# Rows of a block renumbered over the four column tiles of the product with Wu, and the gate's loads issued by GpSimd

## The chip, the cores and the metric

The kernel runs on one core of a Trainium2 chip. Times are device microseconds (us) of that core. A core has a matrix engine (TensorE, PE in the profile; its weight loads are PEld), VectorE (DVE), ScalarE (ACT), GpSimd (POOL) and SyncE (SP). Each engine takes its instructions in the order in which the program lists them. DMA transfers are issued by SyncE, ScalarE or GpSimd. The result of a matmul goes to PSUM; ScalarE or VectorE must read it out before the buffer can be used again.

## The reference

The input x is (32, 8, 256, 256): 32 images of 8 channels. Four layers follow each other, each `x = x + f(group_norm(x))` with 4 groups of 2 channels. The first layer has nearly all the work:

```python
grid = drive                                   # the normalised image
for _ in range(15):
    mapped = 3.9 * grid * (1.0 - grid)
    local = conv3x3(mapped, K_local, groups=8)  # one 3x3 kernel per channel
    grid = 0.85 * (0.7 * mapped + 0.3 * local) + 0.15 * drive
cml = clip(grid, 1e-4, 1 - 1e-4)
h   = relu(conv3x3(x, Wp, bp))                  # 8 -> 128 channels
nca = sigmoid(conv1x1(h, Wu, bu))               # 128 -> 8
g   = sigmoid(conv1x1(relu(conv3x3([x, cml, nca], Wg1, bg1)), Wg2, bg2))
f   = g * cml + (1 - g) * nca
```

Layer 1 is a 3x3 convolution of values rounded to 8 bits, with one scale taken over the whole batch; layer 2 is a 3x3 convolution in float32; layer 3 averages 5x5 windows. All is float32 except the products of layer 1.

## The kernel before

**Two stages.** Layer 0 runs first, for all images, because the scale of layer 1 needs the maximum over the batch; its result goes to `x1_d` in device memory. Layers 1 to 3 follow, image by image, three images in flight.

**Layer 0, the lattice.** `lattice(b, ahead)` makes the 15 steps for image b. Six channels (`CP`) are kept as patches of 16 x 8 pixels on the partitions, in two halves of three channels. A half-step is: three matmuls with `patch_sb` (L367), three with `ring_sb` on the neighbouring patches' edges (L369), then on VectorE a step to take the result out of PSUM (L377) and one to form `v * (v - 1)` (L383), and four DMAs (`spread`, L245, SyncE) that copy the edges to `rings`. The other two channels are computed on VectorE alone: they lie in `strip`, four rows to a partition, and nine multiply-adds (`tap`, L316) form the 3x3 sum. Six of the nine (dy = 1 and 0) stand in the first half-step and three (dy = 2) in the second; at its end `own`, the inner rows of `strip`, is written (L395) and two DMAs (`edges`, L249 and L250) bring the rows above and below from the neighbours. The `psc` results share three PSUM buffers.

**Layer 0, the rest.** `gated()` makes the 128-channel product, the one with Wu, and the gate. An image is cut into 16 blocks of 16 rows, and one n stands for two blocks (row r of both, 512 columns, in one matmul), so an image has eight n. `load(n, half)` brings `im`, eight rows with their neighbours, in six DMAs by GpSimd (L474); two `im` buffers are used. A batch is four rows: four matmuls `ph` with `wp_sb` (L602), each taken out by ScalarE as `hh` (L607). After the second `ph` of the next batch, `second()` multiplies those four `hh` with Wu (L580, `pn`). Each of these products has 32 output columns, of which 8 are not zero: row r goes to the 32 partitions of column tile q, at place i within it, with `q, i = divmod(r, 4)`. In the order (0, 4, 1, 5) the four products of a batch use the tiles 0, 1, 0, 1. After 16 rows `close` applies the sigmoid (`nh`, L558) and loads `hb`, the rows next to the block's border, by `beside_blocks`.

`gate(n, quarter)` is cut into pieces, and each batch runs the next piece of each gate that is due. The first piece issues the loads, on ScalarE's queue: `xq` and `cq` (L486) and `ha` (`beside_blocks`, L451) for every second n, `xc` (L492, two DMAs) for each n. Then come three pieces of six `pg` instructions (L506), one with `ha` and `hb` (L511, L512) and a relu, one with `pq` (L517) and a sigmoid, and one with seven VectorE operations and the store of the result (L539, GpSimd).

**The order of the work.** It is written out by hand (`manual_schedule`). `lattice(b)` yields after each half-step a length of time (`BLOCK`, 7.4), and as much of `gated()` of image b − 1, by the lengths that this yields, is put there. After each half-step one item of `errands` follows: stores of the normalised image (`xn_d`, `nr_d`), loads of the next one, and its statistics in the pieces of `stats_parts`. Image 0 has no `gated()` beside it, and that of image 31 stands alone at the end.

**Layers 1 to 3.** The order there is chosen by the framework. `layer2` stores its result to `x3` (L740) and loads it again as `y`, in other places, with 16 DMAs (L747); `layer1` of a later image loads `x1` (L703). All of these are issued by GpSimd.

## Time and profile before

| what | value |
|---|---|
| median of 3 runs | 17682.97 us (17682.23 to 17724.92) |
| profiled execution, own time | 17729.61 us |
| profiled execution, span | 17727.6 us |
| PE busy | 16666.2 us (94%) |
| PEld busy | 6752.9 us (38%) |
| DVE busy | 13279.5 us (75%) |
| ACT busy | 4005.7 us (23%) |
| POOL busy | 2761.8 us (16%) |
| granted TensorE clock, mean | 0.953 |

A line of a group names the source line, the engine, the operation, the tiles written and read, the shapes and the count; then the busy time in us and the mean length in ns; then the time that the engine stood idle just before, and what ended it. Idle time of an engine that is not the bottleneck costs nothing. In the list of waits the numbers are the total in us, the count, and the longest. In a timeline the columns are the start, the length (both us), the engine and the instruction, and in brackets the idle time before it. "ACTq" and "SPq" are the queues' own instructions, DMA issues above all; on POOL the issues are shown as busy time. In the answer by stage the columns are the stretch, its length, the busy time of PE, PEld, DVE, ACT and POOL with the number of instructions, the granted clock, the DMA engines' share and GB/s.

### The profile page before, as it was taken

The page shows a single profiled execution, that of the slowest core. Times are in us where ns is not written, and L with a number is a line of the kernel's source. Part 1 is how long each engine was busy: PE and PEld are TensorE (multiplying, and loading weights), DVE is VectorE, ACT ScalarE, POOL GpSimd, SP SyncE. Part 2 cuts the span into 40 slices and gives each one's busy share as a digit, 9 for nine tenths or more (in the row PEclk, how much of TensorE's full clock was granted, in tenths as well). Part 3 has the DMA queues.
Part 4 walks back from the last instruction along what each step waited for, and adds up shares of the span by engine and source line. Part 5 has one row for each costly group of instructions (what it writes and reads, how often), then busy time and mean ns, then how long its engine had stood idle before and what let it go on. Part 6 is the DMA issues. An engine that isn't in the chain of part 4 may idle for free.

```text
span 17727.6 us, 134114 instructions
## 1 busy us (share of the span) xinstructions
PE 16666.2 (94%) x42888; PEld 6752.9 (38%) x42888; DVE 13279.5 (75%) x17529; ACT 4005.7 (23%) x5982; POOL 2761.8 (16%) x4469
## 2 busy tenths in 40 slices
PE   5999999999999999999999999999999999899999
PEld 2333333333333333333333333333333333344444
DVE  8787777777777887777888777787777885555554
ACT  0222222222222222222222222222222222211110
POOL 0111111111111111111111111111111111111111
PEclk7999999999999999999999999999999999899999
DMA  4666666666666666666666666666666665455554
GB/s 82 125 124 129 128 128 125 126 128 127 129 125 126 131 123 129 124 124 126 127 126 127 130 127 130 128 129 124 131 127 128 128 122 117 113 124 125 131 126 103
DMA packets 846207, 2208.34 MB, mean 125 GB/s; under 512 B 251021, under 2 KB 529781, under 8 KB 761413
## 3 DMA queue, kind: packets, MB, share of 16 engines
q0 software_dynamic: 341504, 1147.07, 33.4%
q1 hardware_dynamic: 352452, 774.38, 21.4%
q10 hardware_dynamic: 151552, 278.31, 6.0%
q8 instruction: 350, 5.73, 0.2%
q14 instruction: 349, 2.85, 0.1%
HBM read 1078.72 MB, written 404.28 MB: 84 GB/s over the span
## 4 chain that ended last, share of the span: by engine, by line
PE 73%; DVE 14%; DMA 9%; issue 2%; ACTq 1%; ACT 1%; POOL 0%; SPq 0%; DVEq 0%; POOLq 0%
PE ph L602 16%; PE psc L367 11%; PE psc L369 11%; PE pg L506 10%; PE pn L580 7%; DVE acc L316 7%; PE psv L771 6%; PE psv L692 5%; DMA strip<-strip 3%; DVE state L383 2%; DVE state L377 2%; DMA ha<-nr_d 2%; PE psv L696 2%; DMA rings<-state 1%; PE psv L775 1%
## 5 line engine op out<-in xcount | busy, mean ns | idle before, releaser
L316 DVE SCALAR_TENSOR_TENSOR acc<-strip,taps_sb,acc 128x1024 f32<-128x1024 f32 x3840 | 4930.8, 1284 | 359.6 <-DMA strip<-strip 243.2
L602 PE MATMUL ph<-im,wp_sb 72*128 72x512 f32 x8192 | 4190.5, 626 | 580.4 <-ACT hh L607 530.8
L607 ACT ACTIVATE hh<-ph,bp_sb 128x512 f32<-128x512 f32 x4096 | 2753.5, 687 | 7094.7 <-PE ph L602 6611.3
L377 DVE SCALAR_TENSOR_TENSOR state<-psc,flat 128x512 f32<-128x512 f32 x2880 | 1900.6, 686 | 2022.1 <-PE psc L369 1736.8
L367 PE MATMUL psc<-state,patch_sb 128*128 128x512 f32 x5760 | 2817.8, 626 | 261.2 <-DVE stat L105 154.2
L369 PE MATMUL psc<-rings,ring_sb 80*128 80x512 f32 x5760 | 2704.8, 606 | 24.4 <-DMA rings<-state 24.2
L474 POOL DMA_DIRECT2D im<-xn_d x3072 | 1726.4, 567 | 5667.5 <-PE ph L602 5580.7
L602 PEld LDWEIGHTS ph<-im,wp_sb 72*128 72x128 f32 x8192 | 1494.1, 194 | 2693.2 <-issue 1872.2
L580 PE MATMUL pn<-hh,wu_sb 128*32 128x512 f32 x8192 | 1979.2, 604 | 0.0
L367 PEld LDWEIGHTS psc<-state,patch_sb 128*128 128x128 f32 x5760 | 1110.3, 199 | 1882.2 <-issue 1145.0
L383 DVE SCALAR_TENSOR_TENSOR state<-state 128x512 f32<-128x512 f32 x2688 | 1689.3, 684 | 0.0
L369 PEld LDWEIGHTS psc<-rings,ring_sb 80*128 80x128 f32 x5760 | 1116.7, 194 | 1466.8 <-issue 1443.0
L771 PE MATMUL psv<-xr,w_sb 128*128 128x512 f32 x2560 | 1160.3, 595 | 0.5 <-DVE xr L756 0.5
L539 POOL DMA_DIRECT2D x_d<-xc x256 | 146.8, 574 | 6493.9 <-DVE xc L534 6493.7
L580 PEld LDWEIGHTS pn<-hh,wu_sb 128*32 128x32 f32 x8192 | 389.1, 109 | 1438.1 <-issue 1438.1
L506 PE MATMUL pg<-xq,wg_sb 128*128 128x512 f32 x1536 | 897.5, 731 | 0.0
L692 PE MATMUL psv<-xh,w_sb 128*128 128x512 f32 x1536 | 703.3, 594 | 8.1 <-DVE xh L728 4.1
L506 PE MATMUL pg<-nh,wg_sb 128*128 128x512 f32 x1536 | 701.3, 592 | 0.0
L506 PE MATMUL pg<-cq,wg_sb 128*128 128x512 f32 x1536 | 701.2, 592 | 0.0
L771 PEld LDWEIGHTS psv<-xr,w_sb 128*128 128x128 f32 x2560 | 475.5, 189 | 565.6 <-issue 561.2
L780 DVE TENSOR_TENSOR y<-psv,y 128x512 f32<-128x512 f32 x256 | 176.5, 690 | 621.6 <-PE psv L775 621.5
L316 DVE SCALAR_TENSOR_TENSOR acc<-strip,taps_sb,d 128x1024 f32<-128x1024 f32 x480 | 613.7, 1278 | 0.0
(147 smaller groups left out, 10893.0 us busy)
## 6 DMA issues: line engine op xcount, KB each, us to landing
im<-xn_d POOLq DMA_DIRECT2D x3072, 193.3 KB, 8.2
rings<-state SPq DMA_DIRECT2D x1920, 159.5 KB
rings<-state SPq DMA_DIRECT2D x1920, 106.3 KB
strip<-strip SPq DMA_DIRECT2D x960, 126.0 KB
xn_d<-xb POOLq DMA_DIRECT2D x128, 516.0 KB, 12.5
nr_d<-xb POOLq DMA_DIRECT2D x128, 516.0 KB, 12.0
xq<-nr_d ACTq DMA_DIRECT2D x128, 516.0 KB
cq<-cr_d ACTq DMA_DIRECT2D x128, 516.0 KB
```

The costliest lines, as they stand in the source:

```text
L316: nc.vector.scalar_tensor_tensor(acc, strip[:, dy : dy + RQ, dx : dx + W], taps_sb[:, 3 * dy + dx : 3 * dy + dx + 1], d2 if dy == 1 and dx ...
L367: nc.tensor.matmul(pss[-1], patch_sb[:, c, :], inner(c), start=True, stop=False)
L369: nc.tensor.matmul(pss[c % HALF], ring_sb[:, c, :], rings[half][:, c % HALF, 0 : TX * SY].rearrange("p (x y) -> p x y", y=SY)[:, :, 0:TY], ...
L377: nc.vector.scalar_tensor_tensor(inner(c), pss[c % HALF], FLOOR, dr[:, c], ALU.max, ALU.add)
L383: nc.vector.scalar_tensor_tensor(v, v, 1.0, v, ALU.subtract, ALU.mult)
L474: nc.gpsimd.dma_start(im[24 * dy : 24 * dy + 24, k, 0:run], window(xn_d[b % 3], at, [[HP * WP, C], [1, 3], [1, run]]),)
L506: nc.tensor.matmul(o, wg1_sb[:, s, dx, :], src[:, :, dx : dx + W], start=s == dx == 0, stop=False,)
L580: nc.tensor.matmul(pn[32 * q : 32 * q + 32, :], wu_sb[:, i, :], hh, start=i == 0, stop=i == 3,)
L602: nc.tensor.matmul(ph.rearrange("p (k w) -> p k w", w=W), wp_sb, im[:, :, j * WP : j * WP + W], start=True, stop=True,)
L607: nc.scalar.activation(hh, ph, AF.Relu, bias=bp_sb)
L692: nc.tensor.matmul(o, w[:, dx, :], src[:, 2 * i : 2 * i + 2, dx : dx + W], start=dx == 0, stop=False,)
L771: nc.tensor.matmul(o, w3_sb[:, dx, :], xr[:, k, 2 * g : 2 * g + 2, dx : dx + W], start=dx == 0, stop=False,)
```

## The change

The rows of a block are numbered anew: row r now goes to column tile r mod 4, at place r // 4 (`i, q = divmod(r, 4)`), and a batch is four rows in turn, so that its four products with Wu name all four column tiles. Everything that is laid out by rows follows: the stores to `nr_d` and `cr_d`, the loads of `xc` and `y`, which now take four rows 4 apart in a DMA, and the weights of the convolutions over rows (`turn`). The gate's loads go from ScalarE's queue to GpSimd's, `beside_blocks` among them. `load` is issued in pieces among the matmuls of the next batch. The taps with dy = 0 go to the second half-step. `stats_parts` pauses once more, before the square root.

```diff
@@ stats_parts
         nc.vector.tensor_scalar(u[:, 0:1], ps2[:, 0:1], 1e-5, None, ALU.add)
+        yield
         nc.scalar.activation(u[:, 1:2], u[:, 0:1], AF.Sqrt)
@@ errands (cr_d in lattice likewise)
-                            nr_d[b % 3], r.start * C * HB * WP,
-                            [[WP, P], [C * HB * WP, 4], [1, WP]],
+                            nr_d[b % 3], r.start // 4 * C * HB * WP,
+                            [[WP, P], [4 * C * HB * WP, 4], [1, WP]],
@@ lattice
-                    for dy in (1, 0) if half == 0 else (2,):
+                    for dy in (1,) if half == 0 else (0, 2):
@@ beside_blocks
-                    nc.scalar.dma_start(
+                    nc.gpsimd.dma_start(
@@ load
+                ims.append(im)
                 for dy in range(3):
                     for k in range(2):
...
+                        yield
-                ims.append(im)
@@ gate
-                        nc.scalar.dma_start(quarter[name], t[b % 3][:, k0 : k0 + 4, :])
+                        nc.gpsimd.dma_start(quarter[name], t[b % 3][:, k0 : k0 + 4, :])
...
                 for k in range(2):
-                    nc.scalar.dma_start(
-                        xc[:, k, :],
-                        window(
-                            x, b * C * H * W + (k0 + k) * RB * W, [[W, RB], [H * W, C], [1, W]]
-                        ),
-                    )
+                    for j in range(4):
+                        at = b * C * H * W + ((k0 + k) * RB + j) * W
+                        nc.gpsimd.dma_start(
+                            xc[32 * j : 32 * j + 32, k, :],
+                            window(x, at, [[4 * W, 4], [H * W, C], [1, W]]),
+                        )
@@ second
-                    q, i = divmod(r, 4)
+                    i, q = divmod(r, 4)
@@ gated
-                    for rows in ((0, 4, 1, 5), (2, 6, 3, 7)):
+                    for rows in ((0, 1, 2, 3), (4, 5, 6, 7)):
...
                             four.append((hh, 8 * half + j))
+                            next(coming, None)
+                            if i % 2 == 0:
+                                next(coming, None)
...
-                    if n + 1 < B * NCH:
-                        load(n + 1, half)
+                    coming = load(n + 1, half) if n + 1 < B * NCH else iter(())
@@ layer2
             for k in range(HB):
-                nc.gpsimd.dma_start(
-                    y[RB * (k % 8) : RB * (k % 8) + RB, k // 8, :, :],
-                    window(x3, k * W, [[C * NPX, RB], [NPX, C], [1, W]]),
-                )
+                for i in range(4):
+                    m = RB * (k % 8) + 4 * i
+                    nc.gpsimd.dma_start(
+                        y[m : m + 4, k // 8, :, :],
+                        window(x3, i * C * NPX + k * W, [[4 * C * NPX, 4], [NPX, C], [1, W]]),
+                    )
@@ laid_out, on_rows
-        return a.reshape(RB * i, 3, RB * o)
+        turn = np.arange(RB) % 4 * 4 + np.arange(RB) // 4
+        return a[turn][:, :, :, turn].reshape(RB * i, 3, RB * o)
```

## The prediction

> **What bounds the kernel now.** I read the share of busy time first, then the matmuls of one image in order of time, then the waits, then the answer by stage.
>
> Page of the kernel before, its groups of instructions:
> ```profile
> L316 DVE SCALAR_TENSOR_TENSOR acc<-strip,taps_sb,acc 128x1024 f32<-128x1024 f32 x3840 | 4930.8, 1284 | 359.6 <-DMA strip<-strip 243.2
> L602 PE MATMUL ph<-im,wp_sb 72*128 72x512 f32 x8192 | 4190.5, 626 | 580.4 <-ACT hh L607 530.8
> ...
> L580 PE MATMUL pn<-hh,wu_sb 128*32 128x512 f32 x8192 | 1979.2, 604 | 0.0
> ```
> TensorE is busy for 94% of the span, VectorE for 75%. TensorE's only large wait is for ScalarE's `hh`. 8192 `pn` instructions at 604 ns each would be 4948 us, yet their union is 1979 us: they overlap. The timeline of TensorE shows how:
> ```profile
> 5006.43 1.91 PE L580 MATMUL pn<-hh,wu_sb 128*32 128x512 f32 x8
> 5008.27 1.13 PE L602 MATMUL ph<-im,wp_sb 72*128 72x512 f32 x2
> 5013.85 2.08 PE L602 MATMUL ph<-im,wp_sb 72*128 72x512 f32 x2 [4.45 <-ACT hh L607]
> 5015.72 3.97 PE L367 MATMUL psc<-state,patch_sb 128*128 128x512 f32 x6
> 5019.52 2.74 PE L369 MATMUL psc<-rings,ring_sb 80*128 80x512 f32 x6
> ```
> A matmul is two instructions. Six `psc` take 2.58 us at full speed (0.43 us each), but eight `pn` take 1.84 us to the next `ph`: in the trace they start in pairs 7 ns apart, a pair each 0.43 us, and 0.13 us is left over. After the wait of 4.45 us the next pair takes 1.87 us instead of 0.86 and six `psc` 3.80 us instead of 2.58: 2.2 us more are lost at a lower clock. What ScalarE does in such a wait (its timeline):
> ```profile
> 5195.94 0.69 ACTq L451 DMA_DIRECT2D ha<-zero  x1
> 5196.67 1.41 ACTq L451 DMA_DIRECT2D ha<-cr_d  x2
> 5199.66 3.44 ACTq L492 DMA_DIRECT2D xc<-in_x  x2
> 5203.15 0.69 ACT L514 ACTIVATE g<-pg,bg_sb 128x512 f32<-128x512 f32 x1 [15.90 <-DMA strip<-strip]
> ```
> It issues the gate's loads, each held by earlier transfers, and `hh` is queued behind them. The other place is the square root. From the list of waits:
> ```profile
> ACT u L114 <- DVE u L112: 867.3, 94, 285.6
> ...
> PE ph L602 <- ACT hh L607: 530.8, 148, 12.6
> ...
> PE psc L367 <- DVE stat L105: 154.2, 30, 9.8
> ```
> Busy time by stage (PE, PEld, DVE, ACT, POOL) for image 0, which has no other work beside it, and for image 11:
> ```profile
> 100.00:300.00 200.00, 126.64 (x219) 49.94 (x220) 197.02 (x233) 0.00 (x0) 0.00 (x0) 0.81 0.34 62
> ...
> 5110.00:5577.00 467.00, 440.26 (x1138) 175.93 (x1138) 370.25 (x462) 115.22 (x173) 74.13 (x121) 0.96 0.63 127
> ```
> VectorE can run at 98.5% and needs 370 us of an image's 467. The images 1 to 31 lie between 440 and 14867 us, 465.4 us each; the part after 15200 us (layers 1 to 3) has TensorE full.
>
> **What the skill says.** The Trainium skill, TensorE: Matmul & The Clock Gate, Part 3 (packing small matmuls): outputs of at most 32 columns in distinct column groups run at the same time, three tiles measured 2.38 times. The trace agrees for two tiles (8 × 0.43 = 3.43 us done in 1.84); nothing here shows four. Same page, Part 1: an idle window of about 3.4 us drops the clock; agrees with the 2.2 us above. DMA: Bandwidth & Descriptors, "Issuing engines are not separate DMA queues": another issuer saves only the sequencer's time. Here that time holds up `hh`. Same page, "Why a DMA increments its semaphore by 16": the slowest dimension limits the engines of a transfer, and GpSimd's smaller transfers go round; so four pieces of 4 rows should load the engines as one of 16 did. No run here shows that yet.
>
> **The change part by part.**
>
> *Four column tiles.* Rows 0 to 3 now go to four different tiles, instead of two tiles alternating. No instruction is added. Eight passes should take two slots: 2 × 0.43 + 0.13 = 0.99 us, 0.86 less (estimate). There are 8192 / 8 = 1024 groups, all on TensorE's own queue: 881 us. Bounds: 0 (only two tiles ever run together) and 881.
>
> *The gate's loads.* Off ScalarE: 2048 issues (128 `xq`, 128 `cq`, 640 `ha`, 640 `hb`, 512 `xc`) of 0.33 to 0.73 us by their medians, some 43 us per image, and the waits inside them. *The new pause* before the square root puts it a half-step later, when its input is made. Together these are the ScalarE waits: 531 us of idle TensorE, and 148 waits × 2.3 us at the lower clock (2.2 above; 2.5 in the wait that ended at 5204) = 340 us; about 30 more at the transposes. Sum 900 us. What is late next: `psc` buffers held by a statistic that VectorE copies behind its taps (154 us now), which remain.
>
> They reappear on GpSimd: `xc` comes in quarters, 2048 pieces, so 1536 + 2048 = 3584 issues, 112 per image, beside 3872 now (121). At the 0.56 us of an `im` load they cost 63 us; where every eighth must wait for a landing of some 8 us, 1 us each. GpSimd is then busy for 136 to 233 us of an image. Queued behind them are the next `im` loads, and behind these `ph`. An `im` half lasts a sixteenth of an image, 26 us, and needs 6 × 0.56 + 8.2 = 11.6 us: 14 us of cover. `xq` is used one batch (13 us) after its issue, `ha` four, `xc` six. I cost this at nothing. Loads of `hb` now hold GpSimd until the sigmoid of `nh` is done, with three `im` pieces behind it, needed 20 us later: nothing. Spreading the `im` issues: same six, nothing.
>
> *Taps of dy = 0 to the second half.* VectorE's work per half-step goes from 11.4 and 9.4 us (image 0) to 7.5 and 13.3. The wait for `strip` (243 us, VectorE only) goes. A half-step on TensorE will be about 12.2 us, so VectorE falls 1.1 us behind in one half and recovers in the other; the cover is that the next `psc` needs only buffers read at the start. Without it: 1.1 × 15 × 31 = 510 us.
>
> *`y` in 64 pieces instead of 16.* In layer 2, GpSimd:
> ```profile
> 16024.64 4.23 POOL L747 DMA_DIRECT2D y<-x_d  x8 [6.53 <-DMA x_d<-x]
> 16030.86 5.34 POOL L747 DMA_DIRECT2D y<-x_d  x8 [1.98 <-issue]
> 16036.56 0.57 POOL L703 DMA_DIRECT2D x<-x_d  x1 [0.36 <-DVE u L119]
> ```
> 64 × 0.53 to 0.72 us = 34 to 46 us, against 11.5; so `x1`'s load, queued behind, leaves 22 to 35 us later. It lands after 21 us, at 16058, and L706 reads it at 16084.5: 27 us of cover. Late by 0 to 8 us, 32 times: 0 to 250 us; I take 20, as the landing is longest beside the `y` loads themselves.
>
> *Stores to `nr_d`, `cr_d`, the permuted weights:* same number and bytes, nothing.
>
> **Sum.** TensorE per image: 465.4 − 881/32 − 900/31 = 409 us. VectorE's floor: 370/0.985 + 17 us of waits at its ends (for `ps` 12.5, for `flat` 4.9) = 393. Two engines so close hinder each other; I add 6 us per image, 190 us. Span: 17727.6 − 881 − 900 + 190 + 20 = 16157. The profiled execution took 17729.6, 47 more than the median of 17683; so 16157 + 2 − 47 = **16110 us**.
>
> **The rivals.**
> - *Two tiles at a time, as now* (the change does not do what it says there). For: the trace shows no more than pairs. Against: the pairs are perfect, so the tiles are independent. Then 16110 + 881 − 190 (VectorE has room) = 16800.
> - *VectorE becomes the bound.* For: 370 us busy, and 13.3 us in one half. Against: 23 us of margin per image (393 to 416). With 430 us per image in place of 415: + 465, 16570.
> - *GpSimd's pace is the bound, and the kernel is slower.* For: 233 issues per image and 64 in layer 2, one queue, each held by the landings before. Place: `x1` behind `y`, period 64p + 8 us against 77 now. At p = 1.9 us it adds 32 × (64 × 1.9 + 8 − 77) = 1690 us, the whole gain, and phase 1 (233p = 443) begins to lose too. Against: `y` goes at 0.72 us with its waits. At p = 2.0: phase 1 back to 465 us, layers 1 to 3 + 1890: about 19500.
> - *`x1` late by 8 us, the rest as forecast:* 16340.
>
> **How the numbers follow.** Chances: as forecast 0.60, two tiles 0.11, VectorE 0.14, `x1` late 0.07, GpSimd's pace 0.08 (of which 0.01 ends at no change). Faster 0.91, same 0.01, slower 0.08; 0.3% is about what a measurement of this kernel can tell from no change. The likeliest case's own range is 15880 to 16450: no hindrance and all of the low clock regained, or three times the hindrance. The range reaches to the two-tile case: 15880 to 16800.
>
> **What would show it.** Eight `pn` in 1.0 us with four starting together (or 1.84: rival one). No `hh` waits of 3 us and more on TensorE, the clock nearer 1.0 in phase 1, no `xc` on ScalarE's queue. VectorE at 88 to 92% in phase 1; if its idle time before L377 vanishes and TensorE waits for `psc` or `state`, rival two. In layers 1 to 3: `y` issues at 0.5 to 0.7 us, TensorE still full; if L706 waits for `x`, the loads are late. I am wrong if TensorE waits for `im` or `xq`, or the second part grows beyond 2530 us by more than 250.

## The result, and the profile after

The changed kernel takes 18377.83 us (median of 4 runs, 18358.49 to 18386.44) against 17701.24 us for the kernel before in the same comparison: a ratio of 1.038, 95% interval 1.0361 to 1.0399. It is 3.8% slower. The forecast was 16110 us with a range of 15880 to 16800, so it has the wrong sign and the time lies far outside the range. The profiled execution has a span of 18384.5 us, 656.9 more than the 17727.6 of before.

Page of the changed kernel, busy time and groups of instructions. The lines of the code have moved: L602 is now L607, L580 is L583, L367 and L369 are L369 and L371, L747 is L756, L756 (`xr`) is L765, L771 and L775 are L780 and L784.
```profile
PE 16615.2 (90%) x42888; PEld 6783.7 (37%) x42888; DVE 13264.9 (72%) x17529; ACT 4120.3 (22%) x5982; POOL 5815.8 (32%) x9589
...
L607 PE MATMUL ph<-im,wp_sb 72*128 72x512 f32 x8192 | 4374.5, 654 | 194.3 <-DMA im<-xn_d 138.9
...
L369 PE MATMUL psc<-state,patch_sb 128*128 128x512 f32 x5760 | 2823.2, 625 | 414.9 <-DVE u L112 333.8
L371 PE MATMUL psc<-rings,ring_sb 80*128 80x512 f32 x5760 | 2884.1, 639 | 176.2 <-DMA rings<-state 176.0
...
L756 POOL DMA_DIRECT2D y<-x_d x2048 | 1307.9, 647 | 683.6 <-DMA y<-x_d 364.9
...
L583 PE MATMUL pn<-hh,wu_sb 128*32 128x512 f32 x8192 | 1184.8, 652 | 0.0
```
`pn` is down from 1979 us to 1185, and the wait for ScalarE's `hh`, 531 us before, is no longer in the list of TensorE's large waits. In its place TensorE waits for `u` (334 us, VectorE), for `rings` (176) and for `im` (139). And `ph`, whose instructions are the same as before, takes 654 ns in the mean instead of 626.

Busy time by stage in the changed kernel, for the stretch of the images 1 to 31 in layer 0 and for layers 1 to 3 (columns: stretch, length, busy time of PE, PEld, DVE, ACT, POOL, granted clock, DMA share, GB/s):
```profile
440.00:14730.00 14290.00, 13415.15 (x35218) 5402.25 (x35217) 11419.17 (x14223) 3655.36 (x5353) 4278.78 (x7194) 0.91 0.64 128
15028.00:18384.00 3356.00, 2704.73 (x6464) 1184.50 (x6463) 1414.24 (x2746) 340.91 (x447) 1343.60 (x2110) 0.88 0.33 92
```
The same two parts of the kernel before:
```profile
440.00:14867.00 14427.00, 13661.21 (x35216) 5444.48 (x35215) 11461.92 (x14222) 3567.16 (x5352) 2283.04 (x3739) 0.95 0.64 127
15200.00:17727.00 2527.00, 2477.88 (x6464) 1100.38 (x6463) 1386.46 (x2746) 316.87 (x448) 359.31 (x574) 0.99 0.50 121
```
So there are two separate disappointments. Layer 0 became only 137 us shorter, where 1590 were forecast. Layers 1 to 3 became 829 us longer, where 20 were forecast.

**An account of layer 0.** The records give, for each trace, the time in which TensorE stood idle (gaps over 0.3 us) and the time at which the granted clock was one half. If what was done at half clock would take half the time at full clock, then length = work + idle + low/2, and the "work" that comes out should depend only on the instructions. (It overstates the clock's share a little, since TensorE is idle in part of the low time.) All kernels of this study are in the table; what each is comes in the next section. Lengths run from the first `ph` beside the lattice to the lattice's last transpose.

| kernel | median us | layer 0: length | idle | low clock | work | layers 1–3 |
|---|---|---|---|---|---|---|
| before | 17701 | 14430 | 766 | 1380 | 12974 | 2527 |
| after | 18378 | 14293 | 873 | 2566 | 12137 | 3357 |
| e1_y_pieces | 18527 | 14407 | 750 | 1363 | 12976 | 3357 |
| e4_34_pieces | 18551 | 14351 | 712 | 1304 | 12987 | 3388 |
| e2_old_layers | 17610 | 14335 | 979 | 2532 | 12090 | 2529 |
| e3_two_tiles | 17415 | 14124 | 557 | 1069 | 13033 | 2532 |
| e5_gp_loads | 17221 | 13926 | 456 | 987 | 12977 | 2529 |
| e6_pad | 16894 | 13630 | 980 | 1053 | 12124 | 2529 |
| e9_before_pad | 17582 | 14282 | 822 | 922 | 12999 | 2530 |
| e11_pause | 17603 | 14297 | 723 | 1204 | 12972 | 2527 |
| e8_taps | 17082 | 13803 | 723 | 1747 | 12207 | 2526 |
| e7_pad_stats | 16750 | 13502 | 911 | 826 | 12178 | 2526 |
| e12_late_xc | 16754 | 13495 | 891 | 856 | 12176 | 2535 |
| e10_all | 16620 | 13376 | 826 | 716 | 12192 | 2530 |
| e13_early_loads | 16701 | 13441 | 901 | 758 | 12161 | 2535 |
| e14_all_two_tiles | 16805 | 13524 | 343 | 302 | 13030 | 2529 |
| e15_no_rows | 17010 | 13768 | 489 | 619 | 12970 | 2531 |

The work column falls into two groups: 12970 to 13033 us where the products with Wu use two tiles at a time, 12090 to 12207 where they use four. The account therefore closes to within 120 us, and the rest of the story can be told in its three terms. For the change: work −837, idle +107, low clock +593 (half of 2566 − 1380), layers 1 to 3 +830, and −35 between the lattice's end and layer 1 (333 us to 298): +658, against 657 measured.

### The profile page after: what moved, and what is told of

It is laid out like the page before. It is cut to its first block, busy times and chain, and to the rows that moved or that the text cites. A ratio compares the mean times of both kernels' runs of the same rounds, so it can differ in the third digit from the quotient of the medians.

```text
span 18384.5 us, 137840 instructions
## 1 busy us (share of the span) xinstructions
PE 16615.2 (90%) x42888; PEld 6783.7 (37%) x42888; DVE 13264.9 (72%) x17529; ACT 4120.3 (22%) x5982; POOL 5815.8 (32%) x9589
## 2 busy tenths in 40 slices
DMA packets 965017, 2210.50 MB, mean 120 GB/s; under 512 B 429196, under 2 KB 633204, under 8 KB 880196
## 5 line engine op out<-in xcount | busy, mean ns | idle before, releaser
L612 ACT ACTIVATE hh<-ph,bp_sb 128x512 f32<-128x512 f32 x4096 | 2813.7, 687 | 8515.1 <-PE ph L607 8456.9
L607 PE MATMUL ph<-im,wp_sb 72*128 72x512 f32 x8192 | 4374.5, 654 | 194.3 <-DMA im<-xn_d 138.9
L369 PE MATMUL psc<-state,patch_sb 128*128 128x512 f32 x5760 | 2823.2, 625 | 414.9 <-DVE u L112 333.8
L371 PE MATMUL psc<-rings,ring_sb 80*128 80x512 f32 x5760 | 2884.1, 639 | 176.2 <-DMA rings<-state 176.0
L607 PEld LDWEIGHTS ph<-im,wp_sb 72*128 72x128 f32 x8192 | 1589.0, 204 | 2497.8 <-issue 2198.1
L369 PEld LDWEIGHTS psc<-state,patch_sb 128*128 128x128 f32 x5760 | 1099.9, 197 | 2020.7 <-issue 1143.9
L371 PEld LDWEIGHTS psc<-rings,ring_sb 80*128 80x128 f32 x5760 | 1162.2, 203 | 1719.9 <-issue 1652.1
L497 POOL DMA_DIRECT2D xc<-in_x x2048 | 1211.8, 595 | 1576.5 <-DMA im<-xn_d 723.4
L756 POOL DMA_DIRECT2D y<-x_d x2048 | 1307.9, 647 | 683.6 <-DMA y<-x_d 364.9
L780 PE MATMUL psv<-xr,w_sb 128*128 128x512 f32 x2560 | 1271.8, 649 | 136.5 <-DVE xr L765 136.5
L583 PE MATMUL pn<-hh,wu_sb 128*32 128x512 f32 x8192 | 1184.8, 652 | 0.0
L780 PEld LDWEIGHTS psv<-xr,w_sb 128*128 128x128 f32 x2560 | 534.7, 210 | 840.5 <-issue 838.2
L453 POOL DMA_DIRECT2D hb<-nh x576 | 318.9, 557 | 1543.8 <-ACT nh L561 1471.2
L509 PE MATMUL pg<-cq,wg_sb 128*128 128x512 f32 x1536 | 774.7, 644 | 0.0
```

Source lines behind the costliest of these rows:

```text
L369: nc.tensor.matmul(pss[-1], patch_sb[:, c, :], inner(c), start=True, stop=False)
L371: nc.tensor.matmul(pss[c % HALF], ring_sb[:, c, :], rings[half][:, c % HALF, 0 : TX * SY].rearrange("p (x y) -> p x y", y=SY)[:, :, 0:TY], ...
L497: nc.gpsimd.dma_start(xc[32 * j : 32 * j + 32, k, :], window(x, at, [[4 * W, 4], [H * W, C], [1, W]]),)
L509: nc.tensor.matmul(o, wg1_sb[:, s, dx, :], src[:, :, dx : dx + W], start=s == dx == 0, stop=False,)
L607: nc.tensor.matmul(ph.rearrange("p (k w) -> p k w", w=W), wp_sb, im[:, :, j * WP : j * WP + W], start=True, stop=True,)
L612: nc.scalar.activation(hh, ph, AF.Relu, bias=bp_sb)
```

## The experiments

Every ratio is to the kernel before in the same comparison, with its 95% interval. Line numbers in a run's lines are those of that run's kernel.

**Layers 1 to 3: is it `y`, and is it GpSimd's pace?** The first kernel is the one before with only the loads of `y` cut into 64 pieces.
```diff
@@ layer2 of the kernel before
-                nc.gpsimd.dma_start(
-                    y[RB * (k % 8) : RB * (k % 8) + RB, k // 8, :, :],
-                    window(x3, k * W, [[C * NPX, RB], [NPX, C], [1, W]]),
-                )
+                for i in range(4):
+                    m = RB * (k % 8) + 4 * i
+                    nc.gpsimd.dma_start(
+                        y[m : m + 4, k // 8, :, :],
+                        window(x3, 4 * i * C * NPX + k * W, [[C * NPX, 4], [NPX, C], [1, W]]),
+                    )
```


> The kernel before with one part of the change alone: y loaded in 64 pieces of four rows instead of 16 of sixteen. Layers 1 to 3 took 2530 us before and 3330 after the change. If the pieces are the cause, whatever their mechanism, this kernel takes 17700 + 800 = 18500 us, and TensorE in the last part waits for xr as in the changed kernel. If the loss of that part comes from something else (the rows' new order, the end of layer 0), it stays within 100 us of 17700.

Measured: 18526.7 us, ratio 1.0474 (1.0458 to 1.0489). Layers 1 to 3 take 3357 us, to the microsecond what they take in the changed kernel; layer 0 is as before. The whole loss of layers 1 to 3 is made by cutting `y`. The second cuts only the first six of the sixteen loads, 34 pieces in all.
```diff
@@ layer2 of the kernel before
+                n = 4 if k < 6 else 1
+                for i in range(n):
+                    r = RB // n
+                    m = RB * (k % 8) + r * i
...
```


> The kernel before with 34 pieces: the first six of the 16 loads of y are cut in four, the other ten are whole. The order that the framework chooses for VectorE and TensorE in layers 1 to 3 is then, instruction for instruction, that of 64 pieces. Theory A (the order is the loss): as with 64 pieces, 18500 us. Theory B (GpSimd's time for the issues is the loss): 18 of 48 extra issues, 17700 + 800 * 18 / 48 = 18000 us.

Measured: 18550.6 us, 1.0492 (1.0475 to 1.051), layers 1 to 3 3388 us. A stretch of layers 1 to 3 in the trace of the kernel with 64 pieces:
```profile
15122.00:18500.00 3378.00, 2699.98 (x6457) 1182.06 (x6456) 1445.10 (x2793) 347.46 (x456) 1366.79 (x2121) 0.87 0.34 92
```
The same stretch in the kernel with 34 pieces:
```profile
15122.00:18500.00 3378.00, 2707.83 (x6455) 1184.29 (x6455) 1412.52 (x2745) 341.40 (x448) 725.40 (x1150) 0.87 0.36 90
```
GpSimd (the fifth busy time) is at work for 1367 us of 3378 in one and for 725 in the other, 40% and 21%, and the loss is no smaller. So it isn't GpSimd's pace. What the two share with the changed kernel, and not with the kernel before, is the order of the instructions: in layers 1 to 3 the framework chooses it. In the traces the order on TensorE, VectorE and ScalarE in e1 and in e4 is instruction for instruction that of the changed kernel, while that of e2 below, which has 16 loads, is that of the kernel before. What the other order does is seen at the start of a layer 3. VectorE in the changed kernel (timeline):
```profile
16520.53 3.76 DVE L765 TENSOR_SCALAR xr<-y,got 128x512 f32<-128x512 f32 x8
16544.30 0.69 DVE L789 TENSOR_TENSOR y<-psv,y 128x512 f32<-128x512 f32 x1 [20.00 <-PE psv L784]
```
TensorE in the changed kernel, same stretch:
```profile
16521.22 11.25 PE L780 MATMUL psv<-xr,w_sb 128*128 128x512 f32 x20 [4.46 <-DVE xr L765]
16542.19 3.78 PE L784 MATMUL psv<-xr,w3h_sb 72*128 72x512 f32 x4 [9.71 <-DMA xr<-xr]
```
All eight `xr` are written in a row right before layer 3 uses them; TensorE waits 4.5 us for the first, runs out of work that doesn't need the halo rows, and waits 9.7 us for the DMA that copies these from `xr`. It comes back at half speed (four `psv` in 3.78 us). Before, VectorE made `xr` in two portions among the work of another image's layer 2 (timeline of the kernel before):
```profile
16051.09 1.45 DVE L756 TENSOR_SCALAR xr<-y,got 128x512 f32<-128x512 f32 x3
...
16077.66 1.44 DVE L756 TENSOR_SCALAR xr<-y,got 128x512 f32<-128x512 f32 x3
```
and TensorE had no gap there. In the changed kernel `xr` is not late for want of `y`: VectorE stands idle ahead of it for 0.2 us in the whole stage. Over the 32 images TensorE's two waits, for the halo rows and for the first `xr`, are 292 and 137 us of the changed kernel, and waits for the small sums of the statistics (105, 63 and 30 us) are most of the rest; TensorE's idle time in the stage is 3356 − 2705 = 651 us instead of 49, and its busy time grew by 227 us at the lower clock: 602 + 227 = 829. The other order with whole loads was not run, so order and cutting are not told apart beyond this; nor does a run show why the framework settles on another order, and from which number of pieces on.

**Layer 0 by itself.** The changed kernel, but layers 1 to 3 laid out as before: `x1` is stored in the old order of rows, in four DMAs, `y` comes in 16 loads, and only the weights `wg1` are turned.
```diff
@@ gate
-                nc.gpsimd.dma_start(x1_d[b][:, bass.ts(r2, 512)], flat)
+                for q in range(4):
+                    nc.gpsimd.dma_start(
+                        window(x1_d[b], q * C * NPX + 512 * r2, [[4 * C * NPX, 4], [NPX, C], [1, 512]]),
+                        flat[32 * q : 32 * q + 32, :],
+                    )
@@ layer2: y as before
@@ on_rows
-        turn = np.arange(RB) % 4 * 4 + np.arange(RB) // 4
+        turn = np.arange(RB) % 4 * 4 + np.arange(RB) // 4 if turned else np.arange(RB)
```


> The changed kernel with layers 1 to 3 as they were: the result of layer 0 is stored to x1 in the old order of rows (four stores instead of one), y is loaded in 16 pieces, the weights of layers 1 to 3 are not permuted. Layer 0 stays as changed. Theory: the 800 us come from y alone and the rest of layer 0's gain was eaten in layer 0: 18378 - 800 = 17580 us, images at 461 us as in the changed kernel. If the last part also slowed layer 0 (GpSimd's queue), images fall toward the 415 us that were forecast, and the time toward 16110.

Measured: 17610.3 us, 0.9958 (0.9944 to 0.9973). Layers 1 to 3 are back at 2529 us. All the rest of the change together gains 0.4%. The four stores are this kernel's own, and they stay in the kernels built on it: TensorE's wait for `xq` rises from 50 us in the changed kernel to 183, its idle time in layer 0 from 873 to 979, and layer 0 is 42 us longer than in the changed kernel. Now two tiles at a time in this kernel:
```diff
@@ gated
-                    for rows in ((0, 1, 2, 3), (4, 5, 6, 7)):
+                    for rows in ((0, 1, 4, 5), (2, 3, 6, 7)):
```


> The same as the kernel with layers 1 to 3 as they were, but the rows of a batch in the order 0, 1, 4, 5 and 2, 3, 6, 7, so that its products with Wu alternate between two column tiles as before the change. A group of eight should take 1.84 us again instead of 1.00. If TensorE's own work sets layer 0's time, this is 1024 * 0.85 = 870 us slower than with four tiles (18450). If TensorE only waits longer for VectorE and the transfers when it is faster, the difference is under 300 us.

Measured: 17415.0 us, 0.9847 (0.9832 to 0.9862). **With four tiles the kernel is 195 us slower than with two.** The table says how: four tiles take 943 us off the work, but idle time rises by 422 us and the time at the lower clock from 1069 to 2532 us, which costs 731.

**Why the clock stays down.** The timeline of TensorE in the changed kernel, after a wait of 5.1 us:
```profile
5545.04 3.75 PE L607 MATMUL ph<-im,wp_sb 72*128 72x512 f32 x4 [5.10 <-issue]
5548.72 1.94 PE L583 MATMUL pn<-hh,wu_sb 128*32 128x512 f32 x8
5550.58 3.78 PE L607 MATMUL ph<-im,wp_sb 72*128 72x512 f32 x4
...
5561.12 1.93 PE L583 MATMUL pn<-hh,wu_sb 128*32 128x512 f32 x8
5562.98 2.08 PE L607 MATMUL ph<-im,wp_sb 72*128 72x512 f32 x2
5564.85 4.97 PE L369 MATMUL psc<-state,patch_sb 128*128 128x512 f32 x6
```
The same, as busy time and granted clock (columns: stretch, length, PE busy, clock, DMA share, GB/s):
```profile
5545.00:5569.00 24.00, 23.96 (x39) 0.50 0.59 103
```
TensorE is busy without a gap for 24 us, and the clock stays at one half all that time; four `ph` take 3.75 us instead of 1.88. It came back only at 5569.3, as the six `psc<-state` ended. The Trainium skill, TensorE: Matmul & The Clock Gate, Part 1, has the clock come back after one busy window of about 3.4 us. The steps in these records are 3.41 us long, as it says, but here six of them, full of matmuls, left the clock where it was, and the seventh, which held nothing but `psc<-state`, ended the low time. So the measurement decides: something in the matmuls counts.

I counted such steps over layer 0, taking those at half clock in which TensorE was busy for 97% of the step and more. In the changed kernel, where matmuls over 128 rows (`psc<-state` and most of `pg`, without `pn`) filled 40% of the step or more, 197 of 214 were the last of their low stretch. Where they filled less than 35%, 5 of 382 were. The rest of such a step is `ph` (72 rows), `psc<-rings` (80), the `pg` of `ha` and `hb` (96 and 72) and `pn`. `pn` in two tiles counts as well: in e3 `pn` filled half or more of 52 of these steps (those under 35%), and all 52 ended the low stretch, among them the 7 in which it filled less than 60%. In four tiles `pn` is through in half the time and fills 57% of a step at most; of 94 such steps with half or more, in the changed kernel and e2 together, 11 did. On average a low stretch lasts 7.0 us in e3 and 11.2 in e2.

If the height counts, zero rows should do. In e2 the 72 rows of `ph` and the 80 of `rings` are filled up to 128 with zeros, in the weights and in the data: the same number of instructions and columns, and the same sums.
```diff
-                im = imp.tile([72, 2, 8 * WP], F32, name="im")
+                im = im2[half]
...
+        im2 = [wt.tile([P, 2, 8 * WP], F32, name=f"im{i}") for i in range(2)]
-        rings = [wt.tile([RING, HALF, SN], F32, name=f"rings{i}") for i in range(2)]
+        rings = [wt.tile([P, HALF, SN], F32, name=f"rings{i}") for i in range(2)]
...
-    ring = np.zeros((RING, CP, P), f)
+    ring = np.zeros((P, CP, P), f)
...
-        wp=inputs["L0_conv_Wp"].transpose(2, 1, 3, 0).reshape(72, P),
+        wp=np.pad(inputs["L0_conv_Wp"].transpose(2, 1, 3, 0).reshape(72, P), ((0, P - 72), (0, 0))),
```


> The changed kernel with layers 1 to 3 as they were, and the products of 72 and 80 rows (ph with wp, psc with ring) made 128 rows high by rows of zeros in weights and data: the same number of instructions and of columns. In the traces the halved clock came back only after a stretch of about 3.4 us with some 40% of matmuls of 128 rows in it, and stretches of ph, rings and pn in four tiles did not bring it back: mean low stretch 11.2 us with four tiles, 7.0 with two. Theory: with 128 rows everywhere each low stretch is 7 us or less; the low time in layer 0 falls from 2532 us to 1400 or less, and the time from 17610 to about 17000. Rival: rows of zeros do not count, or something else holds the clock down: low time and 17610 us unchanged.

Measured: 16893.9 us, 0.9547 (0.9528 to 0.9567), 716 us less than e2. Idle time is the same (979 and 980 us), so that the two fixed `im` buffers which the padding needs changed nothing there, and the work nearly so (12090 and 12124); the low time fell from 2532 to 1053 us, half of which is 740. Of the low steps in which TensorE was busy throughout, counted as above, all 165 were the last of their stretch; in e2 216 of 544 were. After a similar wait in its trace (timeline of TensorE):
```profile
9256.84 3.57 PE L614 MATMUL ph<-im,wp_sb 128*128 128x512 f32 x4 [3.84 <-DMA im<-xn_d]
9260.35 1.09 PE L590 MATMUL pn<-hh,wu_sb 128*32 128x512 f32 x8
9261.36 1.99 PE L614 MATMUL ph<-im,wp_sb 128*128 128x512 f32 x4
```
Four `ph` at half clock, and the next instructions run at full speed. The padding on the kernel before, alone:

> The kernel before with the products of 72 and 80 rows made 128 rows high by rows of zeros, and nothing else changed. If the low clock lasts until a stretch holds enough matmuls of 128 rows, its low time in layer 0 (1380 us in 199 stretches of 6.9 us) falls to stretches of about 5 us, 1000 us, and the time by some 190 us, to 17500. If the padding acts only on pn in four tiles, nothing changes: 17690.

Measured: 17581.7 us, 0.992 (0.9906 to 0.9935): 146 us, with the low time down from 1380 to 922. Padding is worth less here: of the low steps in which TensorE was busy throughout, 198 of 264 already end their stretch in the kernel before, against 216 of 544 in e2.

**The waits: loads, pause, taps, one at a time.** First the kernel before with nothing but the gate's loads moved to GpSimd (`xc` in two loads as before). The edit is shown for `ha` and `hb`; `xq`, `cq` and `xc` have the same.
```diff
@@ beside_blocks
-                    nc.scalar.dma_start(
+                    nc.gpsimd.dma_start(
```


> The kernel before with the gate's loads (xq, cq, ha, hb, xc in two pieces) issued by GpSimd and nothing else changed. Theory of the forecast: ScalarE's waits in those issues go; TensorE's idle time for hh falls from 521 us to about 250 (the square roots stay), with the lower clock after it some 400 us gained: 17300 us. Rival: the loads, no longer held back one by one, fall together and make TensorE wait for rings and xq instead (about 190 us in the changed kernel, and the clock after it): 17600 us or more.

Measured: 17221.1 us, 0.9727 (0.9712 to 0.9742): −482 us. TensorE's list of waits in it:
```profile
PE psc L367 <- DVE stat L105: 217.8, 30, 11.2
PE ph L602 <- ACT hh L607: 121.9, 51, 4.4
```
The wait for `hh` fell from 531 to 122 us, at no cost on GpSimd's side (the wait for `xq` is 4 us in all, for `rings` 30, 24 before). The gain is somewhat above what was expected of this part. The waits of `psc` for statistics grew meanwhile, for `stat` from 154 to 218 us and for `st` from 8 to 100. The pause alone:
```diff
@@ stats_parts of the kernel before
         nc.vector.tensor_scalar(u[:, 0:1], ps2[:, 0:1], 1e-5, None, ALU.add)
+        yield
```


> The kernel before with the pause ahead of the square root alone. Forecast: ScalarE no longer waits for u, which ends about 60 of TensorE's waits for hh, some 230 us idle and 100 us at the low clock: 17690 - 300 = 17400 us. Rival: the wait only moves to psc, whose buffer is held until VectorE has read u behind its taps: less than 100 us gained, and a new wait of psc for u in the trace.

Measured: 17602.7 us, 0.9934 (0.9918 to 0.9951): 125 us by its comparison's medians, where I had counted on some 300. The wait for `hh` fell by 129 us; two others grew from 5 us each, `psc` for `st` (to 57 us) and for `u` (to 35). A `psc` buffer also carries the small sums of the statistics, and it is held until VectorE has read it, which it does behind its taps. In the changed kernel the wait for `u` is 334 us; the theory is that it grew since six taps instead of three now stand ahead of it in the second half-step. Taking the taps back in e2:
```diff
-                    for dy in (1,) if half == 0 else (0, 2):
+                    for dy in (1, 0) if half == 0 else (2,):
```


> The changed kernel with layers 1 to 3 as they were and the taps of dy = 0 back in the first half-step. If the longer second half (13.3 us on VectorE) is what makes psc wait for u, that wait falls from 325 us to under 150 and the time from 17610 by 200 to 350 us; VectorE waits for strip again (some 240 us, not on TensorE's path). If the wait comes from the pause alone, the time stays within 100 us of 17610.

Measured: 17082.2 us, 0.9645 (0.9621 to 0.967), 528 us less than e2 and more than was expected. The line in its list of waits:
```profile
PE psc L369 <- DVE u L112: 85.4, 57, 5.1
```
334 us have become 85, all idle time has fallen by 256, and with the long waits went 785 us of low clock. A part only moved: the waits of `psc` for other statistics (`st`, `stat`) rose from 5 to 131 us, that for `state` from 76 to 159. Another way to the same end: with the padding, the errand (statistics among them) goes ahead of the taps.
```diff
@@ lattice of e6
                         spread(half)
+                    next(ahead, None)
                     for dy in (1,) if half == 0 else (0, 2):
...
-                    next(ahead, None)
                     yield BLOCK
```


> The same, and the errand of each half-step put before the taps in VectorE's order instead of behind them, so that the statistic's copy out of psc's buffer (u, L112 of the changed kernel) waits for 3.6 us of work instead of 11 to 13. TensorE's wait for it (325 us in 60 waits, one half of them from these errands, the other from the gate's own statistics, which do not move) falls to about 170 us: with the clock after each wait, 200 to 300 us faster than without it. Rival: the next psc waits for something else in its place, under 50 us.

Measured: 16749.6 us, 0.9459 (0.9444 to 0.9474): 144 us less than e6. The wait for `u` went from 336 to 151 us, as meant; the gain was below the expectation, because the wait for `rings` rose by 33 us and that for `state` by 49.

**What waits on GpSimd.** In e2, e6 and e7 `pg` waits for `xq` for 177 to 195 us, against 50 in the changed kernel, which has one store of `x1` where these have four, and 4 us in e5. GpSimd in e6 (timeline):
```profile
5135.02 2.39 POOL L543 DMA_DIRECT2D x_d<-xc  x4 [22.52 <-DVE xc L537]
5137.40 3.36 POOL L477 DMA_DIRECT2D im<-xn_d  x6
5140.75 0.59 POOL L489 DMA_DIRECT2D xq<-nr_d  x1
```
TensorE in e6, same place:
```profile
5153.16 5.05 PE L509 MATMUL pg<-xq,wg_sb 128*128 128x512 f32 x6 [5.78 <-DMA xq<-nr_d]
```
`xq` lands 12.4 us after its issue, and the issue is late by the 5.8 us that TensorE waits. GpSimd has stood for 22.5 us at the store of `x1`, for VectorE's `xc`, then issues four stores and six loads of `im`, and only then `xq`. A theory that the eight `xc` loads behind `xq` slow it down would have it cured by issuing them a batch later:
```diff
@@ gate of e7
-                xc = hp.tile([P, 2, W], F32, name="xc", bufs=2)
-                for k in range(2):
-                    for j in range(4):
...
                 yield 0
...
+                    if s == 0:
+                        xc = hp.tile([P, 2, W], F32, name="xc", bufs=2)
+                        for k in range(2):
+                            for j in range(4):
...
                     yield 2.6
```


> The kernel with 128 rows everywhere and the errand ahead of the taps (16750 us), and the eight loads of xc issued one batch later than those of xq, cq and ha. If the burst of loads in one batch is what delays xq and rings (195 and 154 us of TensorE's waits), these fall below 80 and 100 us and the time to about 16550. If they are late for another reason, such as GpSimd held by a wait for the sigmoid or for the store of the result, the time stays within 60 us of 16750.

Measured: 16753.7 us, 0.9454 (0.944 to 0.9468), no change; the wait for `xq` is 186 us after 195. That theory falls. The next edit issues the gate's first loads a batch earlier, in e10 (below):
```diff
                 yield 0
+                yield 0
...
-                due.setdefault(batch + 6, []).append(gate(n, quarter))
+                due.setdefault(batch + 5, []).append(gate(n, quarter))
```


> The kernel with all that helped (16620 us), and the loads of xq, cq and ha issued one batch earlier, so that they stand ahead of the store of x1 of that batch's gate in GpSimd's queue, not behind it. In the traces xq is issued right behind that store, 11 to 18 us before TensorE needs it. Theory: GpSimd, held by the store until VectorE has made the result, is what delays xq: the wait of 134 us falls under 30, with the clock after it 100 to 200 us gained, 16450. If the transfers themselves are slow, the wait stays above 100 us and the time within 50 us of 16620.

Measured: 16701.0 us, 0.9426 (0.9412 to 0.944), 81 us more than e10, and not the 16450 expected. In its list of TensorE's waits `xq` no longer appears, but
```profile
PE ph L616 <- DMA xc<-in_x: 180.6, 38, 8.4
...
PE ph L616 <- DMA im<-xn_d: 122.2, 19, 28.5
```
are there, where e10 has 45 us for `im` and nothing for `xc`. The wait has moved along GpSimd's queue to what is now late on it. (`ph` does not read `xc`; the profile puts the wait down to a neighbour of `im` on the same queue, and I read both lines as lateness of `im`.)

**Together.** e10 is e7 with the taps taken back and `xc` later.

> All that helped together: the changed kernel with layers 1 to 3 as they were, 128 rows everywhere, the errand ahead of the taps, the taps of dy = 0 back in the first half-step, and the loads of xc one batch later than those of xq, cq and ha. Against 16750 us without the last two: the wait for u falls by another 80 us, those for xq and rings by 150, the clock after them returns: 16300 to 16500 us. If the taps' place only mattered through the low clock, it is worth under 100 us here, and the time is that of the kernel with late xc alone.

Measured: **16620.4 us, 0.9377 (0.9363 to 0.9391), faster than both kernels**, 6.2% below before, though above the 16300 to 16500 that were expected. It keeps the whole renumbering in layer 0, four tiles, and all loads on GpSimd. e10 with two tiles at a time, by the same edit as in e3:

> The kernel with all that helped (16620 us), with the products with Wu alternating between two column tiles. Its groups of eight take 1.84 us instead of 1.00: 870 us more work on TensorE. Without the rows of zeros, two tiles were 195 us faster than four. Theory: that was the low clock alone, so with 128 rows everywhere four tiles keep most of their gain: 16620 + 500 to 870 = 17100 to 17500 us. If four tiles hardly help for another reason (VectorE or the transfers set the pace), the two are within 150 us of each other.

Measured: 16804.9 us, 0.9483 (0.9469 to 0.9497). Now four tiles gain 184 us of the 840 that they take off the work, far less than the 500 to 870 expected: the low clock was not all. Idle time rises from 343 to 826 us and the low time from 302 to 716; the largest shares are the waits for `rings` (38 to 150 us), for `xq` (40 to 134) and for `state` (98 to 185). VectorE is busy for 84 to 85% of layer 0 in both. And without the renumbering: the kernel before with the loads on GpSimd, the padding, and the errand ahead of the taps.

> The kernel before with the gate's loads issued by GpSimd (17221 us), 128 rows everywhere and the errand ahead of the taps: no renumbered rows, no pieces, no pause, two column tiles. Low time of 987 us falls by a half or more and the waits of psc for statistics (310 us) mostly go: 17221 - 250 - 250 = 16700 us. If it is as fast as the kernel with all that helped, the renumbering bought nothing; if it stays near 17100, the four tiles are worth some 500 us.

Measured: 17009.8 us, 0.9597 (0.9581 to 0.9613). That is 310 us above the expected 16700; still, three edits that don't touch the numbering give 4.0% of the 6.2.

## Why the prediction was wrong

Its sum against the account, in us of the profiled execution:

| step | forecast | measured | 
|---|---|---|
| four column tiles, work | −881 | −837 |
| lower clock | −340 | +593 |
| waits in layer 0 | −561, +190 for hindrance | +107 |
| layers 1 to 3 | +20 | +830 |
| between layer 0 and layer 1 | 0 | −35 |
| sum | −1572 | +658 |

**Four tiles.** The mechanism and the size held: eight `pn` take 1.00 us at full clock, four starting together. What failed is the step "all on TensorE's own queue: 881 us", that is, that time taken off a queue that is 95% busy comes off the end. In e2 none of it did: against two tiles in the same kernel (e3) it went into waits (+422 us) and half clock (+731). In e10 184 us did.

**"148 waits × 2.3 us at the lower clock = 340 us", all to be regained.** This priced the clock by the number of waits at a fixed 2.2 to 2.5 us each. In these traces the cost of a wait depends on what runs after it. A low stretch lasted 6.9 us on average in the kernel before and some 12 us in the changed kernel, up to 27.3 in the run of its images. In e2 with `pn` in two tiles (e3) it is 7.0, and 52 of some 150 low stretches end on a step filled by half or more with such `pn`; the change halved their time. e6 shows the cause: 716 us for zero rows. Nor was it all of the low clock: by the account the kernel before loses 690 us of layer 0 to it (half of 1380), twice what was booked, so that the low end of the range, for which all of it was to be regained, would lie near 15570 by the same sum (16110 − 190 − 350) and not at 15880. Nothing in the trace of before shows four tiles, so this could not be read there, but the lengths of its low stretches, which differ by what follows, could have been, and were not.

**"`psc` buffers held by a statistic [...] (154 us now), which remain."** They did not remain; the waits of `psc` for statistics grew from 172 us to 339, 334 of them for `u`. I had moved three taps ahead of that very read and priced the move by the buffers that the next `psc` needs "at the start". The pause put the read of `u` under the same taps. e8 shows that this cost 528 us in e2, clock included. The prediction had named 510 as the price without its cover; that the two are close is chance, since its 510 was VectorE falling behind by 1.1 us a step, and not a held buffer.

**"I cost this at nothing" (GpSimd's queue).** Right for e5 and wrong for the change: TensorE waits 139 us for `im` in the changed kernel, 26 before, and 50 for `xq`. I counted GpSimd's issues and the cover of each load, but not that the store of `x1` stands in the same queue and waits for VectorE, 22.5 us in the trace of e6. This could be read in the list of waits of the kernel before (`x_d` is `x1_d`):
```profile
POOL x_d L539 <- DVE xc L534: 6493.7, 253, 46.9
```
What is queued behind a wait is late, however idle the engine is: POOL is 32% busy in the changed kernel. e12 shows that the `xc` loads behind `xq` do not decide, and e13 that an earlier issue ends the wait for `xq` and only moves it to `im`. That moving the store itself would cure it is argued; no run did it.

**"Two engines so close hinder each other; I add 6 us per image."** The image's period is 461 us in the changed kernel, against 409 + 6 forecast, and 431.5 in e10, with most of the other faults mended. What is left there is close to the rival that had VectorE bound at 430, though its reason is not only VectorE (85% busy) but waits for its results, for `rings` and for `xq`, each of a few microseconds.

**"0 to 250 us, I take 20" (`y`).** The slower rival named the right place and the wrong mechanism. Its threshold was an issue of 1.9 us for each piece; the issues took 0.65 us in the mean. Both the forecast and the rival took the order of the instructions in layers 1 to 3 as given. It was not: the framework works it out anew, and the page of before couldn't say how it would. What failed is that the term was priced as a delay in a fixed order; it measured 830 us, waits for `xr` and the clock after them. An unknown of this kind has no bound in the profile; it should have widened the range, and it had no place in it.

**What held.** The wait of `hh` behind ScalarE's issues is gone (−482 us when done alone, with its share of clock; the pause alone −125, together 607 of the 900 that the prediction had for both). The four pieces land no later than the whole: `y` lands 3.2 us after its issue in the median, 6.8 before, so that the fourth of four, at 0.65 us an issue, is in place some 5 us after the first issue (estimate). This agrees with what the prediction took from the Trainium skill's DMA: Bandwidth & Descriptors ("Why a DMA increments its semaphore by 16"), but the transfer engines were also less busy in that stage (0.33 against 0.50), and how evenly the pieces loaded them is not shown. The stores and turned weights cost nothing to be seen. The prediction's own signs had it right as well: it called itself wrong if TensorE waits for `im` or if the second part grows by more than 250 us beyond 2530, and both happened.

## What to carry to other kernels

Where a framework chooses the order, a changed number of DMAs is a changed program: compare the order of instructions before pricing anything in that stage. Price a wait on TensorE with the clock that follows it, and look at how many rows the next matmuls have; filling up those of 72 and 80 rows with zeros added some 30 us of work here and gave 0.8% in the kernel before and 4% in e2. When loads move to an idle engine, read what that engine waits for, not how busy it is.

## What the runs showed of the hardware that was not expected

- The return of the TensorE clock depended here on the kind of matmuls, not on being busy alone. Some steps of 3.41 us at half clock were full of work (97% and more), but had less than 35% of it over 128 rows and `pn` for less than half of the step. In the traces of before, after, e2 and e3 there are 739 of these, and another low step followed every one. With 128 rows in `ph` and `psc<-rings` as well (e6), all 165 full steps ended the low time. That rows of zeros count is shown by the run with padding; that quick `pn` in four tiles count less than slow ones in two is read from the traces only.
- In the changed kernel, with `y` and `xc` loaded in pieces, there are 965017 packets, 846207 before, and 429196 under 512 B, 251021 before; the `y` loads still landed sooner than before (3.2 us after their issue against 6.8).
